# Sixteen layer normalisations: variances by a quarter of TensorE's columns, reciprocals of these alone, and sixteen transfers that spread them

## The chip, the cores and the metric

The kernel runs on one core of one Trainium2 chip. The metric is the device time of one execution in microseconds (us), as the median of several runs. The engines are named as in the profile: PE (TensorE, the matrix array; PEld are its weight loads), DVE (VectorE), ACT (ScalarE), POOL (GpSimd) and SP (SyncE, which here only issues transfers).

## The reference, cut to what matters

The input x has 2 batches of 512 channels and 64x32 = 2048 positions (tokens). Two layers follow each other, all in fp32:

```python
x = _L0_conv_ref(x, Wq, Wk, Wv, Wout, bout)   # 8 heads of 64, softmax attention over 2048 tokens, projection, + x
t = _to_tokens(x)
t = t + _L1_attn_ref(_ln_t(t), ...)           # Nystrom attention: 256 landmarks, 6 pseudo-inverse iterations, convolution of v
t = t + _L1_ffn_ref(_ln_t(t), ...)            # two 512x512 maps, no nonlinearity between them
```

`_ln_t` takes the mean and the variance of each token over its 512 channels and returns (v - m) / sqrt(var + 1e-5). It is applied twice to each of 2 x 2048 tokens. In blocks of 512 tokens these are 16 normalisations: 8 between the layers and 8 ahead of the last map.

## The kernel before

**Layout.** Channels lie on the 128 partitions in four chunks (KC = 4), tokens along the free dimension, in blocks of TB = 512. A sum over channels is therefore a sum over partitions: it is a matmul with the constant matrix `mean_w` (128x128, every element 1/512), which also leaves the sum in every one of the 128 output rows.

**One normalisation (`statistics`, L1183).** Two additions on DVE fold the four chunks into one; a matmul with `mean_w` gives the mean (L1190); DVE subtracts it from the block (L1191); ACT squares (L1194, L1197); DVE adds the squares of the four chunks into one tile of 128x512 (L1202, L1203); a matmul with `mean_w` gives the variance of each token, alike in all 128 rows (L1206); ACT takes sqrt(var + eps) of all 128x512 elements (L1208), and DVE the reciprocal of all of them (L1227 or L1988).

Who uses the result differs. Between the layers (`norm0_steps`), POOL multiplies chunks 2 and 3 by it (L1230), DVE chunks 0 and 1 (L1231), and a transfer stores the block (L1232). Ahead of the last map (class `Finish1`), the block is not multiplied; the map's matmuls (L2022) run on the unscaled block, and DVE multiplies each of their four outputs by the reciprocal (L2011), adds the residual (L2012), and SP stores it (L2013).

**Stages and order.** All engines work through their instructions in order, and the order is written out by hand, as generators that are advanced between each other's steps:

- *First layer's attention* (`attention0`): for each pair of heads, 4 token blocks of 512 times 16 chunks of keys. PE makes scores (L1289), ACT their exponentials (L1297, six buffers), DVE adds them up (L1307), PE multiplies by the values (L1319). At the end of each block, four matmuls of 32 columns each (`ones[:, :Q]`, Q = 32) put the row sums into four groups of 32 partitions of one bank (L805); DVE takes the reciprocal of these 128x256 elements (L1336), `spread` (L816) copies them by eight transfers on SP within SBUF to the rows where they are wanted, and POOL multiplies the output by them (L1339).
- The first batch's output projection (yp_f, L1168, eight matmul passes per block of 128 channels, two banks in turn; its eviction with bias and residual on DVE is L1175) and its four normalisations ("n0_0_0" to "n0_0_3") lie inside the attention of the second batch's first pair, placed by `finish0_units`.
- *Middle phase* (about 1345 to 1470 us): the second batch's projection and its four normalisations, interleaved with the beginning of the second layer by the string ORDER: o is a step of projection, n a step of `norm_of_all`, m a step of the second layer's work.
- *Second layer*: pseudo-inverses (L1866, L1879), landmark attention with scores L1923, exponentials L1928, additions L1932, row sums by the same 32-column matmuls, reciprocal L1952, spread L816, and DVE's product L1959, which the next pair's pseudo-inverse waits behind.
- *End*: `Finish1` for the second batch is placed among the last pairs' attention by TURNS, for the first batch at the very end, with the last of the second, by TAIL. The projection there is yp_g (L1168).

The tile that holds the reciprocals between the layers, "rstd", has one buffer. SP's transfers are issued in the order written, whatever the stage: loads, stores and spreads share its queue.

Of the kernel before, what the change touches and what calls it, by code (L numbers as in the profile page):

```python
# [10 lines left out]
F32 = mybir.dt.float32  # L11
I32 = mybir.dt.int32
AF = mybir.ActivationFunctionType
# [3 lines left out]
P = 128  # L17
# [636 lines left out]
Q = P // 4  # L654
# [2 lines left out]

BAND = P + 2 * HALO

ORDER = "1omnonmmnomomnnm2mnoonmnmnmoomnnm3mnoonmnmmnoomnnmnmmmnmnmmmnmmmmnmnmmmm"  # L660

TURNS = (
    (",,,", "f,,,", "f,,,", "f,,,", "f,", "f,f,f,f,f,"),
# [2 lines left out]
    ("fffoo,,,", "f,f,f,", "f,f,f,", "ff,,oo,", "f,", ",f,,f,f,ff"),  # L666
)

TAIL = "11fffnf11f1ff1afafff1f1f1f1faas11bsbs11bbt"

GAP = object()
REST = object()
# [16 lines left out]
def fast_path(  # L689
# [35 lines left out]
    nc = tc.nc  # L725
    dram = ctx.enter_context(tc.tile_pool(name="dram1", bufs=1, space=bass.MemoryType.DRAM))
    const = ctx.enter_context(tc.tile_pool(name="const1", bufs=1))
    small = ctx.enter_context(tc.tile_pool(name="small1", bufs=2))
# [3 lines left out]
    apool = ctx.enter_context(tc.tile_pool(name="a1", bufs=2))  # L732
# [20 lines left out]
    def chunked(ap):  # L753
        return ap.rearrange("(k p) n -> p k n", p=P)

    def bank(name):
        return ps.tile([P, 512], F32, tag="pp", name=name)
# [21 lines left out]
    def block_of(pool, tag, name):  # L779
        return pool.tile([P, KC, TB], F32, tag=tag, name=name)  # L780

    def row_of(name):
        return apool.tile([P, TB], F32, tag="rinv", name=name, bufs=3)

    mean_w = const.tile([P, P], F32, name="mean_w1")
# [3 lines left out]
    eps = const.tile([P, 1], F32, name="eps1")  # L789
# [390 lines left out]
    def deviation(name):  # L1180
        return apool.tile([P, TB], F32, tag="rstd", name=f"rstd_{name}", bufs=1)

    def statistics(xb, xn, part, name, squares, row, apart=False, back_to_exp=False):  # L1183


        nc.vector.tensor_tensor(part, xb[:, :2, :], xb[:, 2:, :], ALU.add)
        nc.vector.tensor_tensor(part[:, 0, :], part[:, 0, :], part[:, 1, :], ALU.add)
        yield
        mean = bank(f"mean_{name}")
        nc.tensor.matmul(mean, lhsT=mean_w, rhs=part[:, 0, :], start=True, stop=True)  # L1190
        nc.vector.tensor_tensor(xn, xb, mean.unsqueeze(1).to_broadcast([P, KC, TB]), ALU.subtract)  # L1191
        yield
        sq, *others = squares()
        nc.scalar.activation(sq, xn[:, :2, :], AF.Square)  # L1194
        n = 2 // len(others)
        for i, other in enumerate(others):
            nc.scalar.activation(other, xn[:, 2 + i * n : 2 + (i + 1) * n, :], AF.Square)  # L1197
        if apart:
            yield
        for i, other in enumerate(others):  # L1200
            to = sq[:, i * n : (i + 1) * n, :]
            nc.vector.tensor_tensor(to, to, other, ALU.add)  # L1202
        nc.vector.tensor_tensor(sq[:, 0, :], sq[:, 0, :], sq[:, 1, :], ALU.add)  # L1203
        yield
        var = bank(f"var_{name}")
        nc.tensor.matmul(var, lhsT=mean_w, rhs=sq[:, 0, :], start=True, stop=True)  # L1206
        rstd = row()
        nc.scalar.activation(rstd, var, AF.Sqrt, bias=eps, scale=1.0)  # L1208
        if back_to_exp:
            nc.scalar.activation(table, eps, AF.Exp)  # L1210
        yield rstd

    def out0_units(b, t, xb, oTs):

# [3 lines left out]
    def norm0_steps(b, t, xb, xn, part, apart=False, halves=False):  # L1218

        toks = slice(t * TB, (t + 1) * TB)  # L1220
        name = f"n0_{b}_{t}"
        squares = lambda: (xb[:, :2, :], xb[:, 2:, :])
        for rstd in statistics(xb, xn, part, name, squares, lambda: deviation(name), apart, halves):
            yield
        wide = rstd.unsqueeze(1).to_broadcast([P, 2, TB])

        nc.vector.reciprocal(rstd, rstd)  # L1227
        if halves:
            yield
        nc.gpsimd.tensor_tensor(xn[:, 2:, :], xn[:, 2:, :], wide, ALU.mult)  # L1230
        nc.vector.tensor_tensor(xn[:, :2, :], xn[:, :2, :], wide, ALU.mult)  # L1231
        nc.gpsimd.dma_start(chunked(xh_d[b])[:, :, toks], xn)  # L1232
        yield

    def finish0_units(b, oTs, others, outs_done):
# [3 lines left out]
        def later_steps(steps, n):  # L1239
            for _ in range(n):  # L1240
                soon.append(lambda: next(steps, None))
# [15 lines left out]
        for t in range(NTB):  # L1257
            yield from out0_units(b, t, xb, oTs)
            outs_done.append(t)
            xn = block_of(lpool, "xn", f"xn_f0_{b}_{t}")  # L1260
            steps = norm0_steps(b, t, xb, xn, xn[:, :2, :], True, True)
            later_steps(steps, 1)
            yield REST
            for i, n in enumerate(FEW[t]):
                need_soon()
                next(steps)
                yield
                if i and t + 1 < NTB:
                    xb = load(t + 1)
                later_steps(steps, 2)  # L1270
                yield from few(n)
                yield REST
# [689 lines left out]
    class Finish1:  # L1962
# [17 lines left out]
        def steps(self, row, apart=False):  # L1980
            def squares():
                sq = apool.tile([P, 2, TB], F32, tag="acc", name=f"sq_{self.name}")
                return sq, *(row_of(f"sq{k}_{self.name}").unsqueeze(1) for k in (2, 3))

            self.xn = self.xn()
            for rstd in statistics(self.xb, self.xn, self.xn[:, :2, :], self.name, squares, row, apart):
                if rstd is not None:
                    nc.vector.reciprocal(rstd, rstd)  # L1988
                    self.rstd = rstd
                yield  # L1990

        def norm_units(self):
# [382 lines left out]
    def as_block(tile):  # L2375
        return tile.rearrange("p a b -> p (a b)").rearrange("p (k n) -> p k n", k=KC)
# [7 lines left out]
    def norm0(t):  # L2384
        part = apool.tile([P, 2, TB], F32, tag="acc", name=f"part_f0_{t}")
        return norm0_steps(b, t, xbs_[t % 2], xns_[t % 2], part, True)
# [8 lines left out]
    norms, outs = [], []  # L2395

    def norm_of_all():
        for t in range(NTB):
            norms.append(norm0(t))
            for step in range(5):  # L2400
                if step == 2 and t:
                    next(norms[t - 1])
                    yield
                next(norms[t])
                yield
        next(norms[-1])
        yield

    norm = norm_of_all()
    next(norm)  # L2410
    for c in ORDER:
        if c == "m":
# [94 lines left out]
    todo[1].prefetch_w()  # L2507


    halves = small.tile([P, P], F32, name="halves_f", bufs=1)  # L2510
    nc.gpsimd.memset(halves, 0.0)
    nc.gpsimd.memset(halves[:D, :D], 1.0)
    nc.gpsimd.memset(halves[D:, D:], 1.0)
# [27 lines left out]
    for n, pair in enumerate(todo):  # L2541
# [6 lines left out]
        if n == NPAIR + 3:  # L2548

            xb = as_block(kvpool.tile([P, NST, P], F32, tag="v", name="xb_g_early"))  # L2550
            xn = lambda: block_of(lpool, "xn", "xn_g_early")
# [101 lines left out]
    def last_attn1():  # L2653
        pair, ended = todo[-1], []
        pair.attn1_add(0)
        for t in range(NTB):
            for j in range(2 if t else 0):
                pair.attn1_scores(t, j)
                if ended:
                    pair.attn1_end(ended.pop())  # L2660
                if j:
                    pair.attn1_add(t)
                yield
            pair.attn1_values(t)
            yield
            pair.attn1_sums(t)
            pair.attn1_inverse(t)
            ended.append(t)
            yield
# [24 lines left out]
    ones_last = last_attn1()  # L2694
    for c in TAIL:
        if c == "f":
# [27 lines left out]
@with_exitstack  # L2724
def conv_attn_hybrid(
    ctx: ExitStack,
    tc: tile.TileContext,
    x: bass.AP,
    emb: bass.AP,
    freq: bass.AP,  # L2730
    time: bass.AP,
    wq0: bass.AP,
    wk0: bass.AP,
    wv0: bass.AP,
    wo0: bass.AP,
    b0: bass.AP,
    *rest: bass.AP,
):

    nc = tc.nc  # L2740
    keep = ctx.enter_context(tc.tile_pool(name="keep_f", bufs=1))
    bad = keep.tile([P, 1], F32, name="bad")
    bad_i = keep.tile([P, 1], I32, name="bad_i")
    in_order = {mybir.EngineType.PE, mybir.EngineType.DVE, mybir.EngineType.Activation, mybir.EngineType.Pool}
    with tc.manual_schedule(engines=in_order):
        fast_path(tc, x, freq, time, wq0, wk0, wv0, wo0, b0, *rest, bad)
    nc.vector.tensor_copy(bad_i, bad)
    again = nc.values_load(bad_i[:1, :1])
    with tc.If(again > 0):
        general_path(tc, x, emb, wq0, wk0, wv0, wo0, b0, *rest)  # L2750
# [59 lines left out]
```

## Time and profile before

| | |
|---|---|
| median of 3 runs | 2648.89 us (2648.84 to 2649.84) |
| profiled execution | 2649.55 us |
| its span, first to last instruction | 2647.7 us |
| granted TensorE clock, mean | 0.999 |
| ACT busy; POOL busy | 921.0 us (35%); 169.6 us (6%) |
| ACT square roots of L1208, 128x512 | 16 of 687 ns, 11.0 us |
| DVE products L1231, 128x1024 | 8 of 1219 ns, 9.8 us |
| POOL products L1230, 128x1024 | 8 of 3278 ns, 26.2 us |
| PE's longest wait by one cause | 2.8 us (values L1319 for DVE's L1326, 4 times) |

A group row of the profile reads: line, engine, operation, output <- inputs, partitions x elements, count | busy us, mean ns of one | idle time of that engine just before them, and what ended it. A timeline row gives start and duration in us, engine, line, operation, tiles and how many instructions it joins. Waits on an engine are put down to the instruction whose end released them.

### The profile page before, as it was taken

The page shows a single profiled execution, that of the slowest core. Times are in us where ns is not written, and L with a number is a line of the kernel's source. Part 1 is how long each engine was busy: PE and PEld are TensorE (multiplying, and loading weights), DVE is VectorE, ACT ScalarE, POOL GpSimd, SP SyncE. Part 2 cuts the span into 40 slices and gives each one's busy share as a digit, 9 for nine tenths or more (in the row PEclk, how much of TensorE's full clock was granted, in tenths as well). Part 3 has the DMA queues.
Part 4 walks back from the last instruction along what each step waited for, and adds up shares of the span by engine and source line. Part 5 has one row for each costly group of instructions (what it writes and reads, how often), then busy time and mean ns, then how long its engine had stood idle before and what let it go on. Part 6 is the DMA issues. An engine that isn't in the chain of part 4 may idle for free.

```text
span 2647.7 us, 41440 instructions
## 1 busy us (share of the span) xinstructions
PE 2623.1 (99%) x16882; PEld 1353.3 (51%) x16882; DVE 1780.1 (67%) x2259; ACT 921.0 (35%) x1398; POOL 169.6 (6%) x127
## 2 busy tenths in 40 slices
PE   9999999999999999999999999999999999999998
PEld 5343443444344344353344555777677666665444
DVE  5788897886667778767867866544644645465665
ACT  1444453443344434435522323223333232231310
POOL 0011011000001100000002000000000000000000
PEclk9999999999999999999999999999999999999999
DMA  4011011201221201011115633213111112121211
GB/s 147 22 30 36 13 33 49 77 21 52 88 80 58 91 25 32 25 56 60 41 44 182 225 125 118 98 33 129 48 37 61 60 45 100 34 81 36 97 35 49
DMA packets 123608, 177.16 MB, mean 67 GB/s; under 512 B 16784, under 2 KB 77968, under 8 KB 120848
## 3 DMA queue, kind: packets, MB, share of 16 engines
q1 hardware_dynamic: 117264, 153.15, 17.8%
q0 software_dynamic: 5440, 20.97, 2.0%
q8 instruction: 134, 2.20, 0.4%
q14 instruction: 66, 0.54, 0.1%
q10 hardware_dynamic: 704, 0.31, 0.0%
HBM read 94.02 MB, written 63.57 MB: 60 GB/s over the span
## 4 chain that ended last, share of the span: by engine, by line
PE 91%; DVE 6%; issue 1%; ACT 1%; DMA 1%; SPq 0%; DVEq 0%; ACTq 0%
PE av_f L1319 15%; PE sc_f L1289 15%; PE pb L1866 5%; PE pa L1866 5%; PE vp_f L1153 4%; PE yp_g L1168 4%; PE yp_f L1168 4%; PE fp_g L2022 4%; PE vp L1153 4%; PE pc_f L1021 3%; PE pu L2207 3%; DVE acc_f L1307 3%; PE pu_f L1021 2%; PE sc L1695 2%; PE sc L1923 2%; PE av L1716 2%
## 5 line engine op out<-in xcount | busy, mean ns | idle before, releaser
L1297 ACT ACTIVATE p_f<-sc_f 128x1024 f32<-128x1024 f32 x512 | 496.5, 1021 | 540.2 <-PE sc_f L1289 540.0
L1307 DVE TENSOR_TENSOR acc_f<-acc_f,p_f 128x1024 f32<-128x1024 f32 x448 | 575.3, 1284 | 110.8 <-ACT p_f L1297 83.9
L1319 PE MATMUL av_f<-p_f,v_f 64*64 64x512 f32 x4096 | 494.4, 589 | 2.8 <-DVE q_f L1326 2.8
L1289 PE MATMUL sc_f<-q_f,k_f 64*64 64x512 f32 x4096 | 489.9, 591 | 0.3 <-ACT p_f L1297 0.3
L1319 PEld LDWEIGHTS av_f<-p_f,v_f 64*64 64x64 f32 x4096 | 162.5, 133 | 286.8 <-issue 274.3
L1289 PEld LDWEIGHTS sc_f<-q_f,k_f 64*64 64x64 f32 x4096 | 154.2, 133 | 282.2 <-issue 277.2
L1866 PE MATMUL pa<-M 128*128 128x192 f32 (+1 forms) x640 | 150.3, 380 | 0.0
L1866 PE MATMUL pb<-R 128*128 128x192 f32 (+1 forms) x640 | 149.3, 380 | 0.6 <-DVE M L1879 0.6
L1153 PEld LDWEIGHTS vp_f<-wv_f,x 128*128 128x128 f32 x1024 | 115.8, 192 | 5.5 <-issue 5.2
L1866 PEld LDWEIGHTS pb<-R 128*128 128x128 f32 x640 | 106.5, 190 | 23.6 <-DVE M L1879 0.8
L1866 PEld LDWEIGHTS pa<-M 128*128 128x128 f32 x640 | 108.2, 193 | 19.8 <-ACT M L1857 2.0
L1153 PE MATMUL vp_f<-wv_f,x 128*128 128x128 f32 x1024 | 117.9, 276 | 0.0
L1168 PE MATMUL yp_g<-o,wo_f 128*128 128x512 f32 x256 | 113.8, 595 | 0.0
L1168 PE MATMUL yp_f<-q_f,wo_f 128*128 128x512 f32 x256 | 112.4, 595 | 0.1
L1339 POOL TENSOR_TENSOR q_f<-q_f,rinv_f 128x512 f32<-128x512 f32 x32 | 49.0, 1530 | 970.1 <-DMA rinv_f<-acc_f 647.5
L1153 PE MATMUL vp<-w,xh 128*128 128x128 f32 x896 | 105.8, 276 | 0.0
L1153 PEld LDWEIGHTS vp<-w,xh 128*128 128x128 f32 x896 | 102.2, 192 | 5.4 <-issue 3.5
L1879 DVE SCALAR_TENSOR_TENSOR M<-M,pb 128x320 f32<-128x320 f32 (+1 forms) x160 | 60.1, 417 | 60.8 <-PE pb L1866 60.8
L2022 PE MATMUL fp_g<-xn_g,mT 128*128 128x512 f32 (+1 forms) x232 | 99.3, 579 | 0.0
L1928 ACT ACTIVATE p<-sc 128x512 f32<-128x512 f32 x128 | 66.7, 602 | 91.6 <-PE sc L1923 91.1
L1960 POOL TENSOR_TENSOR o<-o,rinv 128x512 f32<-128x512 f32 x32 | 44.4, 1386 | 772.9 <-DVE rinv L1959 587.5
L1879 DVE SCALAR_TENSOR_TENSOR R<-M,pa 128x320 f32<-128x320 f32 (+1 forms) x160 | 58.5, 407 | 42.1 <-PE pa L1866 42.1
(293 smaller groups left out, 3215.9 us busy)
## 6 DMA issues: line engine op xcount, KB each, us to landing
xh<-xh_fd SPq DMA_DIRECT2D x12, 1024.0 KB, 7.9
rinv_f<-acc_f SPq DMA_DIRECT2D x256, 32.0 KB, 1.9
xr_f<-in_x_dram SPq DMA_DIRECT2D x8, 1024.0 KB, 5.2
x_fd<-xr_f POOLq DMA_DIRECT2D x8, 1024.0 KB, 4.7
xh_fd<-xn_f POOLq DMA_DIRECT2D x8, 1024.0 KB, 4.4
k_fd<-kq SPq DMA_DIRECT2D x16, 512.0 KB, 2.6
q_fd<-kq SPq DMA_DIRECT2D x16, 512.0 KB, 3.2
k<-k_fd SPq DMA_DIRECT2D x8, 1024.0 KB, 6.0
```

The lines of the kernel that those rows point to most:

```text
L1021: nc.tensor.matmul(to, lhsT=w[:, k, :], rhs=x[:, k, :], start=start and k == 0, stop=k == 1, skip_group_check=True,)
L1153: nc.tensor.matmul(vp[:, j * P : (j + 1) * P], lhsT=xb[:, k, j * P : (j + 1) * P], rhs=w_of(k), start=k == 0, stop=k == KC - 1,)
L1168: nc.tensor.matmul(yp, lhsT=wo_sb[:, k, m * P : (m + 1) * P], rhs=oTs[k][:, toks], start=k == 0, stop=k == NPAIR - 1,)
L1289: nc.tensor.matmul(sc[r * D : (r + 1) * D, h, :], lhsT=hd.k[rows, lo : lo + D], rhs=hd.q[rows, t * TB : (t + 1) * TB], start=True, stop=True,)
L1297: nc.scalar.activation(p, sc, AF.Exp, scale=D**-0.5)
L1307: nc.vector.tensor_tensor(acc, first if c == 1 else acc, p, ALU.add)
L1319: nc.tensor.matmul(av[r][half, :], lhsT=hd.v[keys, c, half], rhs=pp[keys, h, :], start=c == 0, stop=c == NST - 1,)
L1866: nc.tensor.matmul(dst, lhsT=lhsT[:, k, t * P : (t + 1) * P], rhs=rhs[:, k, :], start=k == 0, stop=k == 1)
L1879: nc.vector.scalar_tensor_tensor(out, m, scale, pr, ALU.mult, ALU.subtract)
L1928: nc.scalar.activation(p[:, h, :], sc, AF.Exp, scale=D**-0.5)
L2022: nc.tensor.matmul(fp[:, cols], lhsT=mT[:, k, m * P : (m + 1) * P], rhs=self.xn[:, k, cols], start=k == 0, stop=k == KC - 1,)
L2207: nc.tensor.matmul(to, lhsT=w[:, k, :], rhs=x[:, k, :], start=start and k == 0, stop=k == 1, skip_group_check=True)
```

## The change

Four things are edited, and the normalisations' arithmetic stays as it was:

1. The variance matmul becomes four, each with 32 columns of `mean_w` as weights and 128 of the 512 tokens as the moving operand. They write four groups of 32 partitions of one bank: rows 32j to 32j+31 hold the variances of tokens 128j to 128j+127. Square root and reciprocal then work on one tile of 128x128, "few".
2. `inverse_deviation` takes the reciprocal of "few" and issues 16 transfers on SP, each of 32 partitions x 128 elements (16 KB), which copy each of the four groups to all four groups of rows of "rstd". There are 16 x 16 = 256 of them in the kernel.
3. Between the layers, the products L1230 and L1231 come one step later than the reciprocal; `norm_of_all` and the string ORDER are rewritten for the additional step.
4. TAIL is rewritten at one place, and the constant tile `halves`, which is used once for a check of bounds, shares the buffer of "few".

On PE, the order of all other work is the same, except for the rearranged middle phase and the places of a few map matmuls under TAIL. The order on POOL is the same. On SP the transfers from "few" to "rstd" are new, each set standing between the loads, stores and spreads of its stage: for the first three normalisations inside the attention ahead of the eight of L816 of that time, for the fourth behind them.

```diff
-ORDER = "1omnonmmnomomnnm2mnoonmnmnmoomnnm3mnoonmnmmnoomnnmnmmmnmnmmmnmmmmnmnmmmm"
+ORDER = "1ommmnonmnomnomnmm2nmmoonmnnmnomonmmmnm3mnoonnnmmnoonnnmmmmnnmnmmnmmmnmmmmmmmn"
...
-TAIL = "11fffnf11f1ff1afafff1f1f1f1faas11bsbs11bbt"
+TAIL = "11fffnf11f1ff1afaff1f11fff1faas11bsbs11bbt"
...
+    def inverse_deviation(rstd, few):
+
+        nc.vector.reciprocal(few, few)
+        for j in range(4):
+            for to in range(4):
+                nc.sync.dma_start(
+                    rstd[to * Q : (to + 1) * Q, j * P : (j + 1) * P], few[j * Q : (j + 1) * Q, :]
+                )
...
-        var = bank(f"var_{name}")
-        nc.tensor.matmul(var, lhsT=mean_w, rhs=sq[:, 0, :], start=True, stop=True)
-        rstd = row()
-        nc.scalar.activation(rstd, var, AF.Sqrt, bias=eps, scale=1.0)
+        var, few = bank(f"var_{name}"), apool.tile([P, P], F32, tag="few", name=f"few_{name}", bufs=1)
+        for j in range(4):
+            nc.tensor.matmul(
+                var[j * Q : (j + 1) * Q, :P], lhsT=mean_w[:, :Q], rhs=sq[:, 0, j * P : (j + 1) * P],
+                start=True, stop=True,
+            )
+        nc.scalar.activation(few, var[:, :P], AF.Sqrt, bias=eps, scale=1.0)
         if back_to_exp:
             nc.scalar.activation(table, eps, AF.Exp)
-        yield rstd
+        yield few
...
+        rstd = deviation(name)
         wide = rstd.unsqueeze(1).to_broadcast([P, 2, TB])
-        nc.vector.reciprocal(rstd, rstd)
-        if halves:
-            yield
+        inverse_deviation(rstd, few)
+        yield
         nc.gpsimd.tensor_tensor(xn[:, 2:, :], xn[:, 2:, :], wide, ALU.mult)
         nc.vector.tensor_tensor(xn[:, :2, :], xn[:, :2, :], wide, ALU.mult)
...
-                    nc.vector.reciprocal(rstd, rstd)
-                    self.rstd = rstd
+                    self.rstd = row()
+                    inverse_deviation(self.rstd, few)
...
-                if step == 2 and t:
+                if step in (1, 3) and t:
                     next(norms[t - 1])
                     yield
                 next(norms[t])
                 yield
-        next(norms[-1])
-        yield
+        for _ in range(2):
+            next(norms[-1])
+            yield
...
-    halves = small.tile([P, P], F32, name="halves_f", bufs=1)
+    halves = apool.tile([P, P], F32, tag="few", name="halves_f", bufs=1)
```

## The prediction

> **What bounds the kernel now.** I read the busy table first, then the chain that ended last, then the groups by shape, the DMA issues and, around single normalisations, the timeline. The page says that TensorE (PE) is the limit, at a granted clock of 0.999:
>
> ```profile
> PE 2623.1 (99%) x16882; PEld 1353.3 (51%) x16882; DVE 1780.1 (67%) x2259; ACT 921.0 (35%) x1398; POOL 169.6 (6%) x127
> ...
> PE 91%; DVE 6%; issue 1%; ACT 1%; DMA 1%; SPq 0%; DVEq 0%; ACTq 0%
> ```
>
> The span is 2647.7 us, so PE idles 24.6 us in all: time is gained only by taking work off PE, and every wait that reaches PE is paid in full. VectorE (DVE) has a third of its time free, so work taken off it is worth nothing by itself. The groups by shape price the parts (busy us, then mean ns of one):
>
> ```profile
> L1336 DVE RECIPROCAL acc_f<-acc_f 128x256 f32<-128x256 f32 x32 | 55.8, 1742 | 0.0
> ...
> L1988 DVE RECIPROCAL rstd_g<-rstd_g 128x512 f32<-128x512 f32 x8 | 26.8, 3350 | 12.8 <-ACT rstd_g L1208 12.8
> ...
> L805 PE MATMUL rs_f<-acc_f,ones 128*32 128x256 f32 x256 | 20.4, 391 | 1.3 <-DVE acc_f L1307 1.3
> ...
> L1206 PE MATMUL var_n<-xr_f,mean_w 128*128 128x512 f32 x16 | 8.7, 623 | 0.0
> ```
>
> **What comes off PE.** A variance is two fp32 passes, and its sixteen in both layers stand at 17.1 us of busy records (8.7 here, 8.4 in the group var_g). Between neighbours of the same shape one occupies the array for 0.86 us, behind a 64*64 matmul 0.96. The new form already exists in this kernel: the attention's row sums put four 32-column matmuls beside each other. In the PE timeline:
>
> ```profile
> 1090.94 0.64 PE L805 MATMUL rs_f<-acc_f,ones 128*32 128x256 f32 x8
> 1091.51 1.98 PE L1021 MATMUL pc_f<-x,wk_f 128*128 128x512 f32 x4
> ```
>
> All eight records (4 groups, 2 passes) of 256 columns take 0.57 us of PE's time, so the four groups do run at once. With 128 columns the two passes are each half as long, but the switches of shape (about 0.115 us each, by the gap at changes of form) and the exposed weight load stay: 0.46 to 0.58 us. The saving is 0.5 us where a 64*64 stands ahead anyway (the four in attention) and 0.28 elsewhere, with some in between; sixteen times, 6.0 us (2.0 in attention, 1.1 in the middle, 2.9 in the last stage). The Trainium skill speaks against this part: "TensorEngine Tiling (Array Packing)", section "Instruction Overhead", says that each matmul carries about 60 cycles and that a factor should not be taken from a dimension that is already small. Were the four run one after another, nothing would be saved (−0); the row of L805 shows eight records ending in 0.57 us although each is recorded with 391 ns, so I take the row.
>
> **What comes off ACT and DVE.** The square root over 128x128 takes about 0.25 us instead of 0.69, the reciprocal by the line through 1742 ns (256) and 3350 (512) about 0.95 instead of 3.35. That is 38 us off DVE, which has 868 us free: 0, except as an earlier start of the spread.
>
> **What is added: 256 transfers on SP.** The nearest row is the spread of the attention's reciprocals (L816), also 32 partitions of SBUF to SBUF, of 1 KB a partition where the new ones have 512 B:
>
> ```profile
> L816 SPq DMA_DIRECT2D rinv_f<-acc_f x256: 507/588/1679, 102.1 to 1356.2; - x128
> ...
> DMA to landing us min/median/max: 1.7/1.9/5.2
> ```
> ```profile
> 909.87 4.96 SPq L816 DMA_DIRECT2D rinv_f<-acc_f  x8
> ```
>
> Eight are issued in 4.96 us, the last itself 0.59, so the pitch is (4.96−0.59)/7 = 0.62 us: SP issues one after another. Sixteen then take 15×0.62 + 1.9 to land + 0.1 to start = 11.4 us, and the spread deviation is ready 0.95+11.4 = 12.4 us after the reciprocal's start (R), instead of 3.35. By size it could be less: 32- to 64-partition transfers with 128 to 512 B a partition are issued in 0.44 to 0.59 us in this trace, which makes the spread 8.5 to 11.4. Here a second rule differs: "DMA: Bandwidth & Descriptors", section "Anatomy of one DMA — SWDGE (gpsimd) path" (the other issue path), puts dispatch at about 50 ns and says that the fixed cost of 2 us is completion latency, so that sixteen issued together would land in about 16×0.05+2 = 2.8 us. The row is of this very queue and says 0.62 per issue. I take 0.62 since 32 partitions are the same.
>
> **Who waits.** Both engines that multiply by the deviation are in order, so what stands behind the multiplication waits too. In the attention's four normalisations the queue on DVE is this (R = 742.75):
>
> ```profile
> 742.75 3.34 DVE L1227 RECIPROCAL rstd_n<-rstd_n 128x512 f32<-128x512 f32 x1
> 746.01 4.46 DVE L1307 TENSOR_TENSOR acc_f<-acc_f,p_f 128x1024 f32<-128x1024 f32 x2
> 750.39 1.21 DVE L1231 TENSOR_TENSOR xn_f<-xn_f,rstd_n 128x1024 f32<-128x1024 f32 x1
> 751.52 2.54 DVE L1307 TENSOR_TENSOR acc_f<-acc_f,p_f 128x1024 f32<-128x1024 f32 x2
> 753.98 0.74 DVE L1175 SCALAR_TENSOR_TENSOR xr_f<-yp_f,b_f,xr_f 128x512 f32<-128x512 f32 x1
> ```
> ```profile
> 746.25 3.14 POOL L1230 TENSOR_TENSOR xn_f<-xn_f,rstd_n 128x1024 f32<-128x1024 f32 x1 [36.24 <-DVE rstd_n L1227]
> ```
> ```profile
> 748.28 0.64 PE L805 MATMUL rs_f<-acc_f,ones 128*32 128x256 f32 x8
> 748.85 14.00 PE L1168 MATMUL yp_f<-q_f,wo_f 128*128 128x512 f32 x32
> ```
>
> The projection yp has two banks: its third block (nominally 748.85 + 7.0 = R+13.1) needs the first one's eviction, L1175. After the change DVE's multiplication waits until R+12.4 (it began at R+7.6); the two additions and the eviction behind it took 4.3 us from its start to the eviction's end, and 2.0 more now, because POOL's half starts at the same moment and an addition beside it runs at about 3.2 us (the 4.46 for two at 746.01) instead of 1.22. The eviction ends at R+18.7, so PE stands for 5.6 us. Three times that is 16.8. For the fourth block the transfers queue on SP behind the eight of L816 shown at 909.87: they are issued from 914.8 and land at 926.2; DVE then stands from 915.3 for about 11 us, the six exponential buffers run out, and PE loses about 5.7. Together +22.5. If the two additions are not slowed, four times 3.8 to 4; if the spread takes 9, each loses 2.4 less.
>
> In the middle phase (1345 to 1470 us) the written order puts the multiplication one step later. By the order of before and after the first is ready at 1405.3 and wanted at 1405.9: 0. The second is wanted at 1433.7 and ready at 1438; the next variance on PE waits about 2.6 for the squares behind it. The last two cost 1 to 3 with POOL's half beside DVE; 2 us of today's waits there go. Net +3.5, between 0 and 8. Other SP transfers (weights, landmark stores) queue behind sixteen issues here, but all are prefetches or stores with tens of us of room: 0, and up to 3 if one is not.
>
> In the last stage, the second layer's batch 1: first normalisation 0. Second: its sixteen transfers come ahead of eight of L816, whose result lands 3.0 us later, and the pseudo-inverse's first product waits for DVE behind it: +3.3. Third: sixteen behind eight, deviation at 2485.9 instead of 2474.8; the output product y (L2011, at 2478.18 now) waits, and the sum of exponentials queued behind it ends at 2488.4, where PE wants it at 2483.4: +5.0. Fourth: only additions with slack, +0.2. Batch 0: the first y moves from 2559.83 to 2554.43+12.4 = 2566.8, the squares' additions behind it end at 2570.2, PE wants them at 2566.1: +4.1. The two next are covered by the 13.7 us of a projection; if the spread exceeded that, PE would pay the rest. At the very end the deviation arrives 13.2 us after the last variance; four pairs of y and addition (8×0.67) end at 18.8 us after it where they now end at 16.5: +2.3. Sum of the last stage +14.9.
>
> **Sum:** −6.0 + 22.5 + 3.5 + 14.9 = +34.9. The profiled execution took 2649.55 us; it becomes 2684.5. The median of the runs (2648.89) lies 0.66 lower, so about 2683.5; I say 2683.
>
> **Rivals.** (a) Cheap issue, the other side: if the smaller transfers are issued at the rule's rate, the spread is 2.8 us, R+3.8, as early as the full reciprocal; then only the 6 us off PE remain: 2643. In between, stalls vanish when the spread is below some 6 us, a pitch under 0.27. Against it stands every row of SP (lowest 0.44). Chance 0.08. (b) The pitch follows size, 0.47: the spread is 9.0; four attention stalls shrink to 3.2, the last stage to about 8, the middle to 1.5: −6+13+1.5+8 = +16, 2665. For it: narrower rows are issued faster. Chance 0.27. (c) The waits are as I say, but the middle phase and the fourth attention block cost their upper ends, and POOL's locked half slows more of DVE: +8 and +5 more, 2696. Chance 0.17. (d) The narrow matmuls bring nothing (run in turn): +6 on the main case, 2689, inside its spread. Chance 0.03. The main case, 0.45.
>
> **Range.** From somewhat below (b) with a little more slack found, 2657, to (c) with (d), 2702. Faster by over 0.2% (5.3 us, about what a measurement of this kernel can tell from no change) 0.08, which is (a); within 0.2% 0.06, the low tail of (b); slower 0.86.
>
> **What would show it.** The variance's records should fall from 17.1 to 5–8 us, DVE's busy time by about 38. SP's issues from few to rstd should show 0.5–0.63 us pitch and 11 us for sixteen. PE should show four waits of 4 to 6 us before yp_f (DVE, L1175) or a score, one before rs, one before var_g, one before pa; DVE waits for DMA rstd of about 5 us each. If the pitch is under 0.3, or DVE's multiplication does not stand still, the forecast is wrong.

## The result, and the profile after

| | before | after |
|---|---|---|
| median of the runs, us | 2649.51 (6 runs) | 2718.24 (6 runs) |
| ratio, 95% interval | | 1.026 (1.0247 to 1.0274) |
| profiled execution; its span | 2649.55; 2647.7 | 2721.58; 2719.8 |
| granted TensorE clock, mean | 0.999 | 0.985 |

The change costs 69 us where 34 were forecast, and the time lies above the forecast range. The profiled execution of after is the slowest of its six, 72.0 us above that of before, so sums of its trace belong to 72.0 us. The page, with the engines' busy times and the chain:

```profile
span 2719.8 us, 41997 instructions
...
PE 2643.9 (97%) x16978; PEld 1358.5 (50%) x16978; DVE 1751.3 (64%) x2259; ACT 917.4 (34%) x1398; POOL 170.2 (6%) x127
...
PEclk9999999999999989999999999999999999999999
...
PE 85%; DVE 8%; SPq 4%; issue 2%; DMA 1%; ACT 1%; DVEq 0%; ACTq 0%
```

Two things are to be seen. PE's idle time went from 24.6 to 75.9 us, because PE waits more; SP's issues, which had 0% of the chain, now have 4%. But PE's busy time went up as well, by 20.8 us, although its work became less. The row of the clock has an 8 in one of its slices where before had only 9s. The waits of PE, largest first (in total, times, longest); a single wait, in which PE runs no matmul, is called a stand below:

```profile
PE yp_f L1168 <- DVE xr_f L1175: 17.9, 3, 6.2
PE sc_f L1300 <- ACT p_f L1308: 8.8, 2, 8.5
PE rs L805 <- DVE acc L1943: 6.9, 1, 6.9
PE av_f L1330 <- DVE q_f L1337: 5.1, 5, 2.3
PE var_g L1216 <- DVE sq_g L1212: 4.0, 1, 4.0
PE var_n L1216 <- DVE xr_f L1175: 3.3, 1, 3.3
PE pb L2218 <- DVE X L1614: 2.7, 1, 2.7
```

Nearly all of these are the waits that were forecast, at the places that were named. The first normalisation inside attention, on DVE and then on SP:

```profile
742.46 0.94 DVE L1185 RECIPROCAL few_n<-few_n 128x128 f32<-128x128 f32 x1
743.32 2.49 DVE L1318 TENSOR_TENSOR acc_f<-acc_f,p_f 128x1024 f32<-128x1024 f32 x2
755.00 1.23 DVE L1242 TENSOR_TENSOR xn_f<-xn_f,rstd_n 128x1024 f32<-128x1024 f32 x1 [9.19 <-DMA rstd_n<-few_n]
756.14 4.69 DVE L1318 TENSOR_TENSOR acc_f<-acc_f,p_f 128x1024 f32<-128x1024 f32 x2
760.75 1.41 DVE L1175 SCALAR_TENSOR_TENSOR xr_f<-yp_f,b_f,xr_f 128x512 f32<-128x512 f32 x2
```
```profile
743.43 10.22 SPq L1188 DMA_DIRECT2D rstd_n<-few_n  x16
```

The reciprocal of 128 columns takes 0.94 us, sixteen issues 10.22 us (0.64 each), and DVE begins its product 12.54 us after the reciprocal's start (forecast 12.4). The eviction L1175 behind it releases PE's third block 19.1 us after that start (forecast 18.7).

What was not forecast stands in the next view: PE's busy time in us, then, as the third value from the end, the granted clock, in five stretches of 3.41 us around the second stand, which lasts from 818.76 to 824.62:

```profile
814.01:817.43 3.42, 3.42 (x10) 1.51 (x9) 0.00 (x0) 0.00 (x0) 0.00 (x0) 1.00 0.11 29
817.43:820.84 3.41, 1.33 (x4) 0.26 (x2) 2.77 (x2) 0.00 (x0) 2.75 (x1) 1.00 0.00 0
820.84:824.25 3.41, 0.00 (x0) 0.00 (x0) 3.31 (x3) 0.00 (x0) 1.45 (x2) 0.50 0.33 135
824.25:827.67 3.42, 3.05 (x4) 1.51 (x5) 0.97 (x2) 0.00 (x0) 0.00 (x0) 0.50 0.42 172
827.67:831.08 3.41, 3.41 (x9) 1.48 (x9) 0.75 (x1) 0.00 (x0) 0.00 (x0) 1.00 0.00 0
```

After a stretch in which PE was busy for 1.33 of 3.41 us the clock falls to exactly half; it stays there through the first stretch of renewed work, in which the view counts 4 matmuls instead of 9 or 10, and returns after it. The trace of after has eleven such times at half clock (slow times) ahead of the last matmul, each 3.4, 6.8 or 10.2 us long, 71.7 us in all, and before had none. In them PE was busy for 52.5 us, so about 26.2 us of work time were lost.

The sum for the profiled execution, with the forecast's terms beside it:

| | measured, us | forecast, us |
|---|---|---|
| PE standing still ahead of its last matmul (65.8, before 16.5) | +49.3 | +38.6 |
| from the last matmul to the end (10.1, before 8.2) | +1.9 | +2.3 |
| variance on PE (before 14.6, from each one's first matmul to the next matmul's start; after 16 x 0.356, and 0.09 each for a switch of form) | −7.4 | −6.0 |
| work at half clock | +26.2 | 0 |
| rest by difference (cause not shown; the new order is one candidate) | +2.0 | 0 |
| sum | +72.0 | +34.9 |

### The profile page after: what moved, and what is told of

It is laid out like the page before. It is cut to its first block, busy times and chain, and to the rows that moved or that the text cites. A ratio compares the mean times of both kernels' runs of the same rounds, so it can differ in the third digit from the quotient of the medians.

```text
span 2719.8 us, 41997 instructions
## 1 busy us (share of the span) xinstructions
PE 2643.9 (97%) x16978; PEld 1358.5 (50%) x16978; DVE 1751.3 (64%) x2259; ACT 917.4 (34%) x1398; POOL 170.2 (6%) x127
## 3 DMA queue, kind: packets, MB, share of 16 engines
q1 hardware_dynamic: 129552, 157.36, 17.9%
## 4 chain that ended last, share of the span: by engine, by line
PE 85%; DVE 8%; SPq 4%; issue 2%; DMA 1%; ACT 1%; DVEq 0%; ACTq 0%
PE sc_f L1300 13%; PE av_f L1330 13%; PE pa L1877 5%; PE pb L1877 5%; PE vp_f L1153 4%; PE yp_g L1168 4%; PE vp L1153 4%; DVE acc_f L1318 4%; SPq L1188 3%; PE pc_f L1021 3%; PE yp_f L1168 3%; PE pu L2218 3%; PE fp_g L2033 3%; PE pu_f L1021 2%; PE sc L1706 2%; PE av L1727 2%
## 5 line engine op out<-in xcount | busy, mean ns | idle before, releaser
L1168 PE MATMUL yp_f<-q_f,wo_f 128*128 128x512 f32 x256 | 120.0, 624 | 18.0 <-DVE xr_f L1175 17.9
L1168 PEld LDWEIGHTS yp_f<-q_f,wo_f 128*128 128x128 f32 x256 | 50.4, 200 | 84.3 <-issue 62.8
```

Of the source, the lines that this page charges most:

```text
L1168: nc.tensor.matmul(yp, lhsT=wo_sb[:, k, m * P : (m + 1) * P], rhs=oTs[k][:, toks], start=k == 0, stop=k == NPAIR - 1,)
```

## Experiments

**Is it the transfers, the narrow matmuls, or the order?** Theory A: what is paid are in-order engines that stand behind sixteen issues on SP, and PE's half clock after each stand. Rival B: the new ORDER and TAIL. Rival C: matmuls of 32 columns count as little activity, so that they lower the clock themselves. The first run keeps only the order:

```diff
-        var, few = bank(...), apool.tile([P, P], F32, tag="few", ...)
-        for j in range(4): ...
-        nc.scalar.activation(few, var[:, :P], AF.Sqrt, bias=eps, scale=1.0)
+        var = bank(f"var_{name}")
+        nc.tensor.matmul(var, lhsT=mean_w, rhs=sq[:, 0, :], start=True, stop=True)
+        few = row()
+        nc.scalar.activation(few, var, AF.Sqrt, bias=eps, scale=1.0)
...
-        for j in range(4): ...
```

> The changed kernel with its new order (ORDER, TAIL, the product one step later), but the variance as one 128x512 matmul, square root and reciprocal over the whole row, and no transfers. Theory A (in-order engines stand behind the spread, and TensorE's clock halves after each such stand): no stand is left, clock 0.999, time within 4 us of the kernel before: 2646 to 2654. Rival B (the new order is to blame for part): slower by its part, 2665 or more. Rival C (narrow matmuls lower the clock): like A here.

Measured: 2659.68 us, ratio 1.0037 (1.0023 to 1.0052); clock 0.998. It lies between: B has a part, 10 us. The waits show it in the middle phase:

```profile
PE sc L1611 <- DVE xn_f L1195: 4.4, 1, 4.4
```

The rewritten ORDER makes a score wait for the subtraction of a normalisation, with the long reciprocals still on DVE; one slow time of 6.8 us follows. None of this run's new waits lies in the last stage, so nothing speaks against TAIL, which was not run by itself. The next run keeps the narrow matmuls and makes the transfers few:

```diff
         for j in range(4):
-            for to in range(4):
-                nc.sync.dma_start(rstd[to*Q:(to+1)*Q, j*P:(j+1)*P], few[j*Q:(j+1)*Q, :])
+            nc.sync.dma_start(rstd[:, j * P : (j + 1) * P], few)
```

> The changed kernel with 4 transfers of 128 partitions in place of 16 of 32. Each copies the whole of few into one block of 128 columns, so most rows of rstd get the deviations of other tokens. Theory A: 4 issues at 0.62 to 0.8 us and 1.9 to land give rstd about 6 us after the reciprocal starts instead of 12.5; the waits in attention go, clock 0.999, and the 7.5 us saved on TensorE show: about 2643 (2640 to 2650). Rival C (the narrow matmuls, not the waits, make the clock fall to half): clock stays near 0.985, 2665 or more.

Measured: 2652.37 us, ratio 1.0006 (0.9999 to 1.0013); clock 0.997. Sixty-six of the 69 us are gone with twelve of sixteen issues, and rival C falls: all narrow matmuls of the 16 variances run as in after. The issue on SP:

```profile
743.30 2.46 SPq L1187 DMA_DIRECT2D rstd_n<-few_n  x4
```

Four transfers of 64 KB are issued in 2.46 us, 0.62 each, where those of 16 KB took 0.64: between these two sizes the price is per issue and not per byte. The result stays some 9 us above the expected 2643, because the fourth normalisation inside attention still stands behind eight other issues (a stand of 2.45 us with 6.8 us of half clock behind it), and the new ORDER has its stand in the middle (1.74 us with 3.4 us of half clock). That puts it outside what A allowed (2650). The wait in the middle:

```profile
PE sc L1616 <- DVE xn_f L1197: 1.7, 1, 1.7
```

The third run spreads in full, with two transfers:

```diff
...
-        for j in range(4): ...
+        few_d = dram.tile([4, P], F32, name=f"few_d_{name}")
+        nc.sync.dma_start(few_d, few[0:P:Q, :])
+        nc.sync.dma_start(rstd, few_d.rearrange("j n -> (j n)").unsqueeze(0).to_broadcast([P, TB]))
```

> The changed kernel with 2 transfers for the spread: one row of each group of few is stored to a scratch in DRAM (2 KB), and one transfer reads it back into all 128 rows of rstd. Nothing is left out. Theory A: about 2.5 us for the store, 3 to 4 for the read with its issue: rstd 6 to 7 us after the reciprocal starts, half of today's; nearly all waits go: 2642 to 2652, clock 0.995 or more. Rival C: 2665 or more. If the read of one line by 128 rows is slow (over 8 us), like the changed kernel, 2700 or more.

Measured: 2653.65 us, ratio 1.0012 (1.0005 to 1.0019). On DVE:

```profile
741.61 0.94 DVE L1185 RECIPROCAL few_n<-few_n 128x128 f32<-128x128 f32 x1
742.47 2.49 DVE L1316 TENSOR_TENSOR acc_f<-acc_f,p_f 128x1024 f32<-128x1024 f32 x2
747.42 1.22 DVE L1240 TENSOR_TENSOR xn_f<-xn_f,rstd_n 128x1024 f32<-128x1024 f32 x1 [2.46 <-DMA rstd_n<-few_d_n]
```

The spread is there 5.8 us after the reciprocal's start, even by way of DRAM and back, and PE no longer stands for yp_f. It ended 1.7 us above what A allowed, at the same two places as the run before: stands of 2.35 and 2.17 us at the fourth normalisation and of 1.74 us in the middle, with 13.7 us at half clock behind them.

**Does a stand alone halve the clock?** The kernel before, with nothing of the change, gets a delay on DVE at the place where after has its wait; a double reciprocal in place gives the value back:

```diff
         if halves:
             yield
+            for n in {0: (64, 64), 1: (128, 128), 2: (256, 256)}.get(t, ()):
+                nc.vector.reciprocal(rstd[:, :n], rstd[:, :n])
```

> The kernel before, with two more in-place reciprocals (of the first 64, 128 and 256 columns, so that the value returns) ahead of DVE's product in the first three normalisations inside attention: a delay of about 1.1, 1.9 and 3.5 us and the product of POOL beside it. No narrow matmul, no transfer. By the eviction's slack TensorE should stand 2.0, 2.8 and 4.4 us, 9 us together. Theory A (the clock halves when TensorE was busy for about half or less of a stretch of 3.4 us): the clock falls after at least the last, and costs about 2 to 3 us for each: 2661 to 2666. Rival C: clock 0.999, only the stands: 2658.

Measured: 2654.87 us, ratio 1.0018 (1.0011 to 1.0025), clock 0.999. The doses were too small to decide: PE stood 0.95 and 2.6 us in the second and third, and lost 0.4 us in the first (the burst of 32 matmuls took 14.41 us instead of 14.00), since DVE came to the product earlier than I had assumed, and the clock did not fall. That already says that a stand of 2.6 us need not lower it. With 288, 400 and 512 columns:

> The kernel before with longer delays than in the run with delays of 1.1 to 3.5 us, which made TensorE stand 0.4, 0.95 and 2.6 us: the double reciprocals now are of 288, 400 and 512 columns (about 3.8, 5.2 and 6.7 us), so stands of about 3.0, 4.5 and 5.9 us, 13.4 together. No narrow matmul, no transfer. Theory A (a stretch of 3.4 us in which TensorE is busy for about half or less halves the clock in the next): the clock halves behind each of the three, 2 to 4 us each: 2669 to 2675. Rival C (the narrow matmuls or the transfers lower the clock): clock 0.999, 2663.

Measured: 2669.37 us, ratio 1.0076 (1.0059 to 1.0092), clock 0.997. PE's waits, and the stretches around the second stand:

```profile
PE yp_f L1168 <- DVE xr_f L1175: 13.1, 3, 5.7
```
```profile
816.87:820.28 3.41, 0.16 (x1) 0.16 (x2) 3.31 (x4) 0.00 (x0) 0.91 (x2) 1.00 0.49 203
820.28:823.69 3.41, 3.41 (x5) 1.33 (x6) 0.44 (x1) 0.00 (x0) 0.00 (x0) 0.50 0.26 105
823.69:827.11 3.42, 3.42 (x10) 1.51 (x9) 0.75 (x1) 0.00 (x0) 0.00 (x0) 1.00 0.00 0
```

Each of the three stands (2.96, 4.35, 5.75 us) is followed by half clock, in which 12.4 us of busy time lost 6.2: 2649.6 + 13.1 + 6.2 = 2668.9, and 2669.4 was measured. In the middle row 5 matmuls end in the time of 10. A delay without transfers and without narrow matmuls pays the same second price, so it belongs to the stand.

**Where does it arise?** Two runs leave parts unchanged. With the four normalisations inside attention in the form of before:

```diff
...
+        if halves:
+            nc.vector.reciprocal(rstd, rstd)
+        else:
             inverse_deviation(rstd, few)
         yield
```

> The changed kernel with the four normalisations inside attention as in the kernel before (128x512 variance, whole reciprocal, no transfers); the other twelve stay changed. Theory A: 28.7 us of stands and 12.0 us of work at half clock (24.1 us of busy TensorE in the slow stretches) go, 2.4 us of saved variance go too: 2718.2 - 38.3 = 2680 (2675 to 2685). If the half clock cost nothing: 2692.

Measured: 2679.94 us, ratio 1.011 (1.0093 to 1.0127), as computed: 38.3 us come from these four. That it agrees so closely is partly luck: between the two profiled executions the difference is 41.9 us, with 17.6 us of half clock in it instead of 12.0, because two of the middle's three stands, which were followed by half clock in after, were not in this run. With only the middle four changed, attention and last stage as before:

> The changed kernel with only its middle four normalisations changed (16 transfers each, new ORDER and TAIL); the four inside attention and the eight of the last stage as before. Theory A: from the changed kernel's trace the middle has 7.6 us of stands (1.33 of them in the kernel before too), 6.8 us lost at half clock, 1.7 us of variance saved and some 2 us of work in a dearer order: 2661 to 2667, which leaves 13 to 19 us of the whole loss for the last stage. If the middle were nearly as cheap as the order alone (2659.7), 2660 or less.

Measured: 2661.65 us, ratio 1.0037 (1.0026 to 1.0049), with runs from 2656 to 2664. The middle, its order included, is worth 11.4 us (2661.65 against 2650.21 beside it), with a scatter of 8; the order alone was 10.0 in the first run. What is left for the last stage is 2679.94 − 2661.65 = 18.3, a difference of two runs and not a run of its own. The profiled execution of this run was one of the shorter ones (2656.64; the three short ones had a mean clock of 0.999, the four long ones 0.996 or 0.997):

```profile
core 0: 2654.8 us, clock 0.999
```
```profile
PE var_n L1221 <- DVE xr_f L1175: 3.3, 1, 3.3
PE pb L2226 <- DVE X L1622: 2.7, 1, 2.7
PE sc L1627 <- DVE xn_f L1200: 1.6, 1, 1.6
```

These are the middle's three stands of after, to a tenth of a us, but here none of them lowered the clock, while in after all three did. For the longest, the stretches between which the clock can change, first in after and then in this run:

```profile
1483.03:1486.44 3.41, 0.70 (x9) 0.45 (x10) 3.34 (x6) 0.21 (x1) 0.00 (x0) 1.00 1.02 362
1486.44:1489.86 3.42, 3.42 (x5) 1.35 (x4) 3.39 (x5) 0.16 (x1) 0.75 (x1) 0.50 0.99 270
```
```profile
1440.70:1444.12 3.42, 1.89 (x5) 0.57 (x3) 3.42 (x4) 0.00 (x0) 1.42 (x2) 1.00 0.35 132
1444.12:1447.53 3.41, 1.62 (x11) 0.83 (x12) 3.34 (x5) 0.37 (x1) 0.72 (x1) 1.00 1.01 309
```

In after the stand of 3.3 us lies almost wholly in one stretch, in which PE was busy for 0.70 us. Here the boundary cuts it in two, and PE was busy for 1.89 and 1.62 us of them.

**Can the wait be taken away?** First by a second issuing engine:

```diff
-                nc.sync.dma_start(
+                (nc.scalar if to % 2 else nc.sync).dma_start(
```

> The changed kernel with its 16 transfers issued half by SP, half by ACT. Nothing is left out. Theory A (what is paid is the issue, 0.64 us each, one after another on one engine): two engines issue side by side, so 8 x 0.64 + 1.9 + 0.95 gives rstd 7.9 us after the reciprocal starts, about where the product stood before; the waits in attention shrink from 6 to about 1 us and most slow clock goes: 2652 to 2662. Rival D (what is paid is the landing or the engines that move the data, shared by both queues): rstd still after 12 us, 2705 or more, and ACT's exponentials late on top.

Measured: 2711.83 us, ratio 1.0235 (1.0218 to 1.0252): a miss. Theory A was right that the issues go side by side, and wrong about the time, because ACT is an in-order engine as well:

```profile
743.73 5.49 ACTq L1188 DMA_DIRECT2D rstd_n<-few_n  x8
749.60 1.94 ACT L1308 ACTIVATE p_f<-sc_f 128x1024 f32<-128x1024 f32 x2 [7.49 <-DMA rstd_n<-few_n]
```
```profile
PE sc_f L1300 <- ACT p_f L1308: 23.2, 5, 6.0
```

SP issued its eight in 5.17 us from the same moment on, and POOL began its product 7.95 us after the reciprocal, so rival D falls too, although the time is the one it named. But an exponential stood behind ACT's eight issues (the row names the landing, which an exponential does not need; the issues end just before it), and PE's next score waited for the exponential: the wait of yp_f for DVE (17.9 us) is gone, and one of 23.2 for sc_f has taken its place. Four more waits for ACT, of 5.7 to 7.7 us, stand in the middle and the last stage. Second, by a later product:

```diff
         inverse_deviation(rstd, few)
         yield
+        if halves:
+            yield
...
-                later_steps(steps, 2)
+                later_steps(steps, 2 + (i == len(FEW[t]) - 1))
```

> The changed kernel with the product of the four normalisations inside attention one group (about 3.4 us of scores and values, and a burst of projection) later; all 16 transfers on SP stay. Theory A: TensorE's stands of 5.9, 5.9 and 6.2 us and the slow clock behind them (12 us with the fourth) vanish where DVE reaches the product after the landing; the fourth, behind eight other transfers, may keep half: 2678 to 2692. Rival D or a wait that only moves: 2710 or more.

Measured: 2736.7 us, ratio 1.033 (1.0313 to 1.0347): a miss, slower still. PE's wait, and DVE's behind it:

```profile
PE mean_n L1199 <- DVE xn_f L1196: 40.2, 3, 13.8
```
```profile
767.78 1.22 DVE L1244 TENSOR_TENSOR xn_f<-xn_f,rstd_n 128x1024 f32<-128x1024 f32 x1
768.92 2.55 DVE L1320 TENSOR_TENSOR acc_f<-acc_f,p_f 128x1024 f32<-128x1024 f32 x2
781.13 1.22 DVE L1195 TENSOR_TENSOR xn_f<-xr_f 128x1024 f32<-128x1024 f32 x1 [9.66 <-DMA xh_fd<-xn_f]
```

The product itself waits no longer. One group later, however, is behind the burst of projection, 24.9 us after the reciprocal (742.91); POOL's half then stood behind the attention's own spread, the block was stored late, and the next normalisation waited for the buffer that the store was reading. The wait had only moved, and became longer.

Last, the change where a spread of two transfers is covered by other work, and the form and ORDER of before elsewhere (the fourth inside attention and the middle four):

```diff
+        full = not halves or t == NTB - 1
...
+        if full:
+            nc.vector.reciprocal(rstd, rstd)
+        else:
+            inverse_deviation(rstd, few, name)
+        if halves:
             yield
```

> Eleven of the sixteen normalisations changed: the first three inside attention and the eight of the last stage, with the spread as 2 transfers through DRAM and the new TAIL; the fourth inside attention and the four in the middle as before, with the old ORDER. Nothing is left out. Theory A: in the run with all sixteen through DRAM TensorE stood only for the fourth and in the middle, so here no stand beside those of the kernel before is left; saved are 3 x 0.61 us and 8 variances of the last stage, 3.7 us: 5.5 us, 2644 (2642 to 2647), clock 0.999. If the variance's saving is taken back elsewhere (weight loads, banks): 2649 to 2651.

Measured: 2644.27 us against 2650.21 beside it, ratio 0.9977 (0.9967 to 0.9986), clock 0.999. It beats both kernels, by 5.9 us where 5.5 were computed. Its page and its longest waits:

```profile
PE 2618.9 (99%) x16948; PEld 1351.3 (51%) x16948; DVE 1757.3 (66%) x2259; ACT 918.0 (35%) x1398; POOL 169.9 (6%) x127
```
```profile
PE av_f L1338 <- DVE q_f L1345: 2.8, 4, 1.0
PE rs_f L805 <- DVE acc_f L1326: 1.8, 3, 0.9
```

PE is busy 4.2 us less than before, and no stand of over 1.6 us is left. The profiled execution is 4.6 us shorter than that of before: besides these 4.2 us, the end after the last matmul is 1.8 us shorter (6.3 for 8.2), and 1.5 us more of waits go the other way, mostly 1.4 us for the first load. So the variances give most of the gain, and the shorter spread at the very end a part.

## Why the prediction was wrong, point by point

- *TensorE's saving* was right in kind and low in size: a quarter-column variance took 0.356 us from its first matmul to the next one's start in 13 of 16 cases (the others held a wait or half clock), with some 0.09 more to switch from a 128*128 form; forecast were 0.46 to 0.58. Together 7.4 us instead of 6.0.
- *The spread's duration* held: 12.54 us against 12.4. The 50 ns for a dispatch that the prediction quotes from the Trainium skill, "DMA: Bandwidth & Descriptors", section "Anatomy of one DMA — SWDGE (gpsimd) path", belong to the other issue path and do not describe this queue: an issue of these spreads took 0.61 to 0.65 us on SP and 0.69 on ACT. The "lowest 0.44" for SP was misread: the trace of before has issues of 0.32 us (L977). The read from DRAM in the run with two transfers took 0.31. Both are still above the 0.27 of rival (a).
- *DVE*: its reciprocals fell by 38.4 us, as forecast, but its busy time by 28.8, since other records grew. Its waits ahead of the product were 9.2 us and not 5, because DVE comes to it earlier: the reciprocal is shorter, and the two additions behind it are no longer slowed by POOL (2.49 us for 4.46). This changed nothing for PE, since the product waits for the landing either way.
- *The three stands in attention* held (5.85, 5.86, 6.18 us for 5.6). *The fourth* was mis-sized: 8.5 and 2.3 us for 5.7. I had DVE at work until 5.6 us after the reciprocal's start; it had only two additions before the product and was done after 3.3 us, so it stood for 14.5 us instead of 11, and then POOL's half slowed two of the additions it had to catch up with (4.69 us for two, the row at 756.14 shows the same). For additions that are not slowed, the prediction's "3.8 to 4" should read 3.6 (5.6 less 2.0).
- *The middle*: its stands of 3.3, 2.7 and 1.6 us, less 1.3 us of waits that went, are +6.2 for +3.5, inside the "between 0 and 8"; another 6.8 us were lost at half clock. The prediction gave the rewritten order no cost of its own. Alone, with the long reciprocals, it costs 10.0 us by the score's wait of 4.4 us; but with short reciprocals this wait is 1.7 us in the runs with four and two transfers, and 1.6 in after. In those two runs the stand of 3.3 us is absent and that of 2.7 is 0.4, so these belong to the sixteen transfers, and the 10.0 us can't be taken for the order's part in after.
- *The last stage*: 2.8 (1.8 and 1.0), 6.9 and 4.0 us of stands and 1.9 us at the end, for 3.3, 5.0, 4.1 and 2.3. Right, with the third normalisation's too small.
- **The step that failed** is "a wait that reaches PE is paid in full", by which I set PE's loss equal to its stand. A stand of several us is paid a second time: 26.2 us of work at half clock in the profiled execution (somewhat less in the other five, whose mean clock is 0.987 or 0.988 and not 0.985), for which the sum had nothing, and the largest of its errors; the stands themselves were 10.7 us larger than forecast. The trace of before does show that the clock falls, at a place where it costs nothing. Its last matmul ends at 2639.56, and in the last 4.5 us, which are all that lowers its mean to 0.999, the clock is half:

```profile
2639.80:2643.20 3.40, 0.00 (x0) 0.00 (x0) 1.41 (x4) 0.00 (x0) 0.00 (x0) 1.00 0.26 82
2643.30:2647.60 4.30, 0.00 (x0) 0.00 (x0) 0.00 (x0) 0.00 (x0) 0.00 (x0) 0.50 0.03 8
```

The Trainium skill has a rule for it: "TensorE: Matmul & The Clock Gate", section "HAM oscillation — how this bites in real kernels", warns of idle gaps over some 3.4 us. The runs agree for the long stands, and show that shorter ones, from 1.5 us on, can be enough. I forecast seven stands of 3.3 to 5.7 us and did not hold them against it. An estimate in hindsight: with the 3.4 to 6.8 us at half clock that most of the slow times above last, half of which is lost, behind each of the seven, the sum would have been 7 x 1.7 to 3.4 = 12 to 24 us higher: 2695 to 2707, and the upper end of the range (2702) as much higher.

## What to carry to other kernels

Count a spread by its issues, here 0.62 us each and one after another on the issuing engine, and put the landing of the last beside the first instruction that needs it; then follow what is queued behind that instruction up to TensorE. Where a stand of TensorE comes out at several us, add 2 to 3 us for the work at half speed behind it: here every stand of 3.9 us or more cost more than its length, and those of 1.5 to 3.3 us did or did not, by where they lay. Moving such a wait to another in-order engine or behind the next burst moves it and removes nothing; fewer issues, or leaving out the places without cover, does.

## What the runs showed of the hardware that was not expected

- The clock falls and returns at multiples of 3.413 us: in after the first slow time begins at 759.40 us and a late one at 2431.93, 490 x 3.4133 apart, and all others fit. It can last beyond the stand by one or two such stretches.
- Every stand of 3.9 us or more, in all kernels, was followed by half clock. Of those between 1.5 and 3.3 us some were (among them 1.57, 1.74, 2.27, 2.45, 2.71, 2.96 and 3.3 us) and some were not (among them 1.57, 2.56, 2.71 and 3.3 us), so less than a whole idle stretch can be enough, and the length alone does not decide.
- What nearly decides is PE's busy share within one stretch of that grid. Each of the twelve traces (before, after and the ten runs) was cut at its own grid, and the stretches at full clock were counted. Where PE was busy for less than 0.40 of the stretch, the next one was at half clock in all 36 cases; between 0.40 and 0.65, in 6 of 37; above 0.65, in 1 of 9195 (0.75, in the run of the middle only). In between the exact condition stays open: a stretch with 0.57 was followed by half clock in the run through DRAM, and one with 0.48 was not in the run of the middle only.
- So equal stands give unequal times, by where the grid cuts them. The run of the middle only scatters by 8 us, 2656 to 2664, and its long executions have the lower mean clock; that their stands are the same is likely but not shown, since one of the seven was traced.
